# Second attention of a gated cross-attention block: the last keys' products of two head groups issued together

## The chip, the cores and the metric

The kernel runs on one core of one Trainium2 chip. The metric is the device time of one execution in microseconds (us); lower is better. Three timed runs of the kernel before gave 1540.47, 1540.97 and 1542.29 us; their median, 1540.97 us, is the time that counts. A separate execution was recorded by the hardware profiler, and every row quoted here comes from it.

## The reference, cut to what matters

The model adds four blocks to `x` (4 batches, 512 tokens, width 512, all float32): an attention, a mixture of experts, a second attention and a second mixture of experts. The change lies in the second attention. It has 16 heads of 32 columns over 512 context rows; the first 496 are ordinary keys, and the last 16 (`DCA`) form an attention of their own, with a softmax of their own, whose result is added:

```python
kv_dca = (y_dca @ Wkv_dca + bkv_dca).reshape(b, DCA, 2, H, HD)
k_dca = _ln(kv_dca[:, :, 0], kn_dca_w, kn_dca_b)
v_dca = kv_dca[:, :, 1]
...
ctx = _attn(qT, k.transpose(0, 2, 1, 3), v.transpose(0, 2, 1, 3))
ctx_dca = _attn(qT, k_dca.transpose(0, 2, 1, 3), v_dca.transpose(0, 2, 1, 3))
ctx = ctx + DCA_WEIGHT * ctx_dca
return ctx @ Wo + bo
```

## The kernel before, in words

The 16 heads are worked in four groups `g` of four heads, so a group fills 128 partitions. A slot is one batch `b`, one group `g` and one block `c` of 128 keys: 4 x 4 x 4 = 64 slots. TensorE does each slot in this order: `exponents` (`sc`, the scores of the slot, four products of 32 rows side by side; ScalarE makes `pt` from them), `weighted` (`o`, values times the `pt` of the slot before), some steps of other jobs, `maxima` of five slots ahead (`m`, scores again, from which VectorE takes the negated row maxima `nm`, two reductions, L1554), and more steps of other jobs. `sc` and `m` share one tag of PSUM tiles (two tiles of two banks each), so the first half of `sc` waits for the first `nm` reduction of the `m` before it, and its second half for the second. `acc` on GpSimd (L1595, L1598) sums the `pt` of a group over its four blocks.

The other jobs are Python generators. The table `WHEN` says at which half slots each is advanced; an even number is the place before `maxima`, an odd one the place behind it. At each place `go` advances every job twice, first the vector parts, then the products. All four engines issue in the order written (`manual_schedule`), so an instruction that waits holds everything behind it on its engine. The jobs share three single PSUM banks through `bank(name)` (`open_psum("psum1", 3)`): a fourth tile waits until the readers of one of the three have finished. Jobs that matter here: `queries` (`q`, `qT`, `d`), `keys`, `values`, `normed` (its transposes `xlnT`), `shared` (the shared expert's `gu` and `po`), `output` (`y`) and `normalized`.

`normalized(b, g)` finishes a group in seven places, 8, 9, 10, 11, 12, 15 and 16 half slots after the group's first slot: the sums `s` of the exponents, a copy, two reciprocals, the multiplication on GpSimd (L1636), then at place 15 (behind `maxima`) the product `dv` (L1641) and at place 16, in the next slot, VectorE's `scalar_tensor_tensor` (L1649), which adds `dv` and a bias to `q_t[:, g, :]`. `dv` is one float32 product with 64 contraction rows: the shares `pd_t` of the last keys are stored so that even groups lie on partitions 0 to 63 and odd groups on 64 to 127. `output` multiplies all four groups of `q_t` by `Wo` after the batch's last group.

Of the kernel before, what the change touches and what calls it, by code (L numbers as in the profile page):

```python
# [14 lines left out]
ALU = mybir.AluOpType  # L15
# [3 lines left out]
P = 128  # L19
# [60 lines left out]
C_BV = C_RMS + NC  # L80
# [6 lines left out]
def kernel(  # L87
# [32 lines left out]
    nc = tc.nc  # L120
# [14 lines left out]
    def bank(name):  # L135
        return phase[0].tile([P, 512], FP, tag="bank", bufs=phase[1], name=name)
# [18 lines left out]
    cols_sb = const.tile([P, N_COLS], FP, tag="cols", name="cols_sb")  # L155
# [375 lines left out]
    with tc.tile_pool(name="att0", bufs=2, reuse_waits="tile") as wk:  # L531
# [228 lines left out]
        b = B - 1  # L760
# [124 lines left out]
    vd_bd = wp1.tile([P, B, D], FP, tag="vd_bd", name="vd_bd")  # L885
# [337 lines left out]
    with tc.tile_pool(name="att1", bufs=1, reuse_waits="tile") as wk:  # L1223
# [18 lines left out]
        def nothing():  # L1242

            yield
            yield
# [372 lines left out]
        def normalized(b, g):  # L1618
            it = batches[b]
            q = it.q_t[:, g, :]  # L1620
            yield
            ps = bank(f"s_{b}_{g}")
            for j in range(4):
                nc.tensor.matmul(
                    ps[j * HD : (j + 1) * HD, :], lhsT=ones, rhs=it.acc[g][:, j, :], start=True, stop=True
                )
            yield
            rs = wk.tile([P, S], FP, tag="rs", name=f"rs_{b}_{g}")
            nc.scalar.copy(rs, ps)
            yield from nothing()  # L1630
            nc.vector.reciprocal(rs[:, : S // 2], rs[:, : S // 2])
            yield from nothing()
            nc.vector.reciprocal(rs[:, S // 2 :], rs[:, S // 2 :])
            yield from nothing()

            nc.gpsimd.tensor_tensor(q, q, rs, ALU.mult)  # L1636
            yield from nothing()
            rows_of = slice(g % 2 * 64, g % 2 * 64 + 64)
            yield
            pv = bank(f"dv_{b}_{g}")  # L1640
            nc.tensor.matmul(  # L1641
                pv,
                lhsT=vd_bd[rows_of, b, g * P : (g + 1) * P],
                rhs=it.pd_t[rows_of, g // 2, :],
                start=True,
                stop=True,
            )
            yield
            nc.vector.scalar_tensor_tensor(  # L1649
                q, pv, cols_sb[:, C_BV + g : C_BV + g + 1], q, ALU.add, ALU.add  # L1650
            )
            yield from nothing()

        def output(b, t):
# [76 lines left out]
        with tc.manual_schedule(engines={E.PE, E.DVE, E.Activation, E.Pool}):  # L1731
# [15 lines left out]
            for k, b in itertools.product(WHEN, range(B)):  # L1747
                first = per * b
                f = first - per
                if k == "normalized":  # L1750
                    for g in range(NC):
                        plan(first + g * TB, WHEN[k], normalized(b, g))
# [20 lines left out]
                elif k == "shifted":  # L1773
                    for g in range(NC):
                        f = first + g * TB
# [55 lines left out]
    with tc.tile_pool(name="exp1", bufs=1, side="right", reuse_waits="tile") as wk:  # L1831
# [60 lines left out]
        with tc.tile_pool(name="route1", bufs=1, reuse_waits="tile") as rp:  # L1892
# [50 lines left out]
            for h in range(8):  # L1943
                k, i0 = h // 4, h % 4 * n
# [4 lines left out]
                for i in range(n):  # L1949
                    nc.tensor.matmul(  # L1950
                        pi,
                        lhsT=hot_r[:, i, :],
                        rhs=hot_c[:, i].rearrange("p z s -> p (z s)"),
                        start=(h == 0 and i == 0),
                        stop=(h == 7 and i == n - 1),
# [145 lines left out]
```

## Time and profile before

| | |
|---|---|
| median of 3 runs | 1540.97 us (1540.47 to 1542.29) |
| profiled execution, its own time | 1549.78 us |
| its span, first to last instruction | 1548.0 us |
| TensorE busy | 1467.6 us (95%), granted clock 0.961 on average |
| VectorE, ScalarE, GpSimd busy | 647.3, 460.4, 577.7 us |
| the 16 `dv` products, busy | 18.0 us, first at 769.0 us, last at 1234.6 us |

The profiled execution is 8.81 us longer than the median of the runs. The page gives busy time by engine, the chain of work that ended last and the costliest groups; the trace answers with instructions in order of time (start, duration, engine, line, operation, tiles; in brackets the idle time before it and what ended it), with waits, and with busy time and granted TensorE clock for stretches of time. A float32 product shows as two matrix-multiply records. Records of matrix multiplies overlap a little at their ends, so the time that one takes in the queue is read from its start to the start of the next.

### The profile page before, as it was taken

What the parts mean: (1) busy time and instruction counts of PE and PEld (TensorE: products, weight loads), DVE (VectorE), ACT (ScalarE), POOL (GpSimd) and SP (SyncE); (2) the same over time, 40 slices, a digit from 0 to 9 for tenths busy, and PEclk for the clock granted to TensorE, in tenths of its full rate; (3) what the DMA queues carried; (4) which work ended last, traced back from release to release, by engine and by line L of the source; (5) the groups of instructions that cost most, each with busy time, mean ns of one, the idle gap of its engine ahead of it and who ended that gap; (6) DMA issues with size and microseconds to landing.
All of it is one profiled execution on the core that took longest, in us unless ns stands there. A gap on an engine that the chain in (4) does not pass through costs nothing.

```text
span 1548.0 us, 15460 instructions
## 1 busy us (share of the span) xinstructions
PE 1467.6 (95%) x5728; PEld 713.2 (46%) x5728; DVE 647.3 (42%) x1244; ACT 460.4 (30%) x722; POOL 577.7 (37%) x488
## 2 busy tenths in 40 slices
PE   7999899999999999798989999999999998899996
PEld 2454366665665666353233333333334354444443
DVE  3764422323312210255575566566654337222221
ACT  2553211111211111144454444543625211122221
POOL 0000121222232221136558576575665510344442
PEclk7999999999999999899999999998899998999998
DMA  9313424452443422410000000000000128444543
GB/s 329 106 75 132 137 44 115 109 133 62 106 136 69 116 63 34 117 69 15 0 1 1 0 1 14 27 2 1 28 28 21 61 108 328 102 87 93 94 88 46
DMA packets 60084, 119.89 MB, mean 77 GB/s; under 512 B 10401, under 2 KB 12961, under 8 KB 58977
## 3 DMA queue, kind: packets, MB, share of 16 engines
q0 software_dynamic: 17024, 40.17, 14.0%
q1 hardware_dynamic: 35872, 64.86, 12.1%
q10 hardware_dynamic: 7104, 13.78, 2.4%
q8 instruction: 49, 0.80, 0.2%
q14 instruction: 35, 0.28, 0.1%
HBM read 80.90 MB, written 37.89 MB: 77 GB/s over the span
## 4 chain that ended last, share of the span: by engine, by line
PE 80%; POOL 6%; DVE 4%; DMA 4%; issue 2%; ACT 2%; SPq 0%; POOLq 0%; ACTq 0%; DVEq 0%
PE gu_s L1117 18%; PE y_s L1134 8%; PE gu_s L408 8%; PE sc L1532 5%; PE m L1532 4%; PE y_s L432 4%; PE y L1268 3%; PE xm L651 3%; PE q L1268 3%; PE o L1608 3%; PE gu L1268 2%; POOL acc L1598 2%; ACT pt L1590 1%; PE v L1268 1%; PE k L1268 1%
## 5 line engine op out<-in xcount | busy, mean ns | idle before, releaser
L1554 DVE TENSOR_REDUCE nm<-m 128x2 f32<-128x992 f32 x128 | 146.3, 1185 | 142.4 <-PE m L1532 142.3
L1590 ACT ACTIVATE pt<-sc 128x1024 f32<-128x1024 f32 (+1 forms) x128 | 124.8, 1021 | 180.9 <-PE sc L1532 162.9
L1143 POOL DMA_INDIRECT sum<-y_s,idx x40 | 63.3, 1582 | 287.7 <-ACT y_s L1142 272.0
L1598 POOL TENSOR_TENSOR acc<-acc,pt 128x2048 f32<-128x2048 f32 (+1 forms) x32 | 144.4, 4511 | 60.7 <-ACT pt L1590 60.7
L1117 PE MATMUL gu_s<-h_t_s,wg 128*128 128x384 f32 (+1 forms) x512 | 150.8, 438 | 1.3 <-DVE h_t_s L1107 0.8
L1117 PE MATMUL gu_s<-h_t_s,wu 128*128 128x384 f32 (+1 forms) x512 | 148.3, 433 | 0.0
L1134 PE MATMUL y_s<-wd,mid_t_s 128*128 128x512 f32 x320 | 143.6, 592 | 0.0
L1128 DVE TENSOR_TENSOR mid_t_s<-act_s,gu_s 128x256 f32<-128x256 f32 (+1 forms) x64 | 31.2, 488 | 257.4 <-ACT act_s L1127 257.4
L408 PE MATMUL gu_s<-wgu,h_t_s 128*128 x288 | 132.1, 602 | 0.0
L1093 POOL DMA_INDIRECT got_s<-table,idx x40 | 40.0, 1001 | 230.6 <-PE lora_d L495 174.9
L1117 PEld LDWEIGHTS gu_s<-h_t_s,wu 128*128 128x128 f32 x512 | 97.7, 191 | 40.4
L1117 PEld LDWEIGHTS gu_s<-h_t_s,wg 128*128 128x128 f32 x512 | 94.9, 193 | 37.4 <-DVE h_t_s L1107 1.2
L1532 PE MATMUL sc<-xT,k_t 32*128 32x512 f32 (+1 forms) x512 | 100.2, 671 | 10.1 <-DVE nm L1554 7.7
L1595 POOL TENSOR_TENSOR acc<-pt,pt 128x2048 f32<-128x2048 f32 x16 | 72.2, 4512 | 94.8 <-ACT pt L1590 94.8
L1127 ACT ACTIVATE act_s<-gu_s 128x256 f32<-128x256 f32 (+1 forms) x64 | 27.9, 437 | 264.9 <-PE gu_s L1117 264.9
L437 POOL DMA_INDIRECT out<-y_s,idx x36 | 57.0, 1584 | 122.1 <-ACT mid_t_s L426 114.5
L1134 PEld LDWEIGHTS y_s<-wd,mid_t_s 128*128 128x128 f32 x320 | 60.9, 190 | 63.8 <-issue 57.6
L1532 PE MATMUL m<-k_t,xT 32*128 32x496 f32 x512 | 88.7, 674 | 1.7 <-ACT pt L1590 1.7
L408 PEld LDWEIGHTS gu_s<-wgu,h_t_s 128*128 128x128 f32 x288 | 52.9, 194 | 53.3 <-issue 53.3
L1608 PE MATMUL o<-pt,v 128*32 128x512 f32 (+1 forms) x512 | 73.4, 647 | 0.0
L432 PE MATMUL y_s<-wd,mid_t_s 128*128 x144 | 67.8, 593 | 0.8 <-ACT mid_t_s L426 0.8
L1142 ACT ACTIVATE y_s<-y_s,w_s 128x512 f32<-128x512 f32 x40 | 27.5, 687 | 121.6 <-PE y_s L1134 118.8
(370 smaller groups left out, 2099.3 us busy)
## 6 DMA issues: line engine op xcount, KB each, us to landing
wg<-in_wg SPq DMA_DIRECT2D x8, 1024.0 KB, 6.2
wu<-in_wu SPq DMA_DIRECT2D x8, 1024.0 KB, 7.0
wd<-in_wd SPq DMA_DIRECT2D x8, 1024.0 KB, 5.4
table<-xln SPq DMA_DIRECT2D x32, 256.0 KB, 2.0
wgu<-in_wgu ACTq DMA_DIRECT2D x2, 4096.0 KB, 15.4
ctx<-in_ctx_t SPq DMA_DIRECT2D x8, 512.0 KB, 6.8
x_sb<-in_x SPq DMA_DIRECT2D x4, 1024.0 KB, 13.9
sum<-x_sb SPq DMA_DIRECT2D x16, 256.0 KB, 2.0
```

The lines of the kernel that those rows point to most:

```text
L408: nc.tensor.matmul(gu[:, k * n : (k + 1) * n], lhsT=t.h_t[:, c, :], rhs=t.gate_up(c)[k], start=(c == 0), stop=(c == NC - 1),)
L432: nc.tensor.matmul(py, lhsT=t.mid_t[:, f, :], rhs=t.down(f), start=(f == 0), stop=(f == nf - 1))
L1117: nc.tensor.matmul(gu[:, k, :n], lhsT=w[:, c, f * P : (f + 1) * P], rhs=g.h_t[:, c, :n], start=(c == 0), stop=(c == NC - 1),)
L1134: nc.tensor.matmul(py, lhsT=g.mid_t[:, f, a * P : (a + 1) * P], rhs=wd[:, f, :], start=(f == 0), stop=(f == F0 // P - 1),)
L1143: nc.gpsimd.indirect_dma_start(out=sum0[:, :], out_offset=bass.IndirectOffsetOnAxis(ap=slots_of(g, a), axis=0), in_=y, in_offset=None, com ...
L1268: nc.tensor.matmul(pp, lhsT=lhs(c), rhs=w[:, c, :], start=(c == 0), stop=(c == n - 1))
L1532: nc.tensor.matmul(halves[j // 2][:n, j % 2, :width], lhsT=lhs(rs), rhs=rhs(rs), start=True, stop=True,)
L1554: nc.vector.tensor_reduce(it.nm[g][:, t, 2 * k : 2 * k + 2], m[:, :, :S2], AX.X, ALU.max, negate=True)
L1590: nc.scalar.activation(it.pt[:n, 2 * k : 2 * k + 2, :], sc[:n], AF.Exp)
L1595: nc.gpsimd.tensor_tensor(acc, it.pt0, it.pt, ALU.add)
L1598: nc.gpsimd.tensor_tensor(acc[:n], acc[:n], it.pt[:n], ALU.add)
L1608: nc.tensor.matmul(it.po[j * HD : (j + 1) * HD, :], lhsT=it.v[:n, c, h * HD : (h + 1) * HD], rhs=pt[:n, j, :], start=(c == 0), stop=(c == ...
```

## The change

Groups are finished in pairs. For an even `g` the generator keeps its places but issues neither product nor addition. For an odd `g` it issues at place 15 the products of `g - 1` and `g` one behind the other, each into its own bank, on rows 0 to 63 and 64 to 127 of the array, and at place 16 the two additions. The number of instructions stays as it was; only the order on TensorE and VectorE and the lifetime of the banks differ.

```diff
-            rows_of = slice(g % 2 * 64, g % 2 * 64 + 64)
-            yield
-            pv = bank(f"dv_{b}_{g}")
-            nc.tensor.matmul(
-                pv,
-                lhsT=vd_bd[rows_of, b, g * P : (g + 1) * P],
-                rhs=it.pd_t[rows_of, g // 2, :],
-                start=True,
-                stop=True,
-            )
-            yield
-            nc.vector.scalar_tensor_tensor(
-                q, pv, cols_sb[:, C_BV + g : C_BV + g + 1], q, ALU.add, ALU.add
-            )
+            yield
+            both = []
+            for k in (g - 1, g) if g % 2 else ():
+                rows_of = slice(k % 2 * 64, k % 2 * 64 + 64)
+                pv = bank(f"dv_{b}_{k}")
+                nc.tensor.matmul(
+                    pv,
+                    lhsT=vd_bd[rows_of, b, k * P : (k + 1) * P],
+                    rhs=it.pd_t[rows_of, k // 2, :],
+                    start=True,
+                    stop=True,
+                )
+                both.append((k, pv))
+            yield
+            for k, pv in both:
+                q = it.q_t[:, k, :]
+                nc.vector.scalar_tensor_tensor(
+                    q, pv, cols_sb[:, C_BV + k : C_BV + k + 1], q, ALU.add, ALU.add
+                )
             yield from nothing()
```

## The prediction, made before the changed kernel was run

> **What bounds the kernel now.** I read the page's busy times and chain first, then the waits of TensorE in the stretch of the second attention (755 to 1240 us), then the rows of `dv`, then all 16 places of `dv` in order of time.
>
> ```profile
> PE 1467.6 (95%) x5728; PEld 713.2 (46%) x5728; DVE 647.3 (42%) x1244; ACT 460.4 (30%) x722; POOL 577.7 (37%) x488
> PE 80%; POOL 6%; DVE 4%; DMA 4%; issue 2%; ACT 2%; SPq 0%; POOLq 0%; ACTq 0%; DVEq 0%
> PE sc L1532 <- DVE nm L1554: 7.7, 8, 3.8
> L1641 PE MATMUL dv<-pd_t,vd_bd x32: 589/641/694, 769.0 to 1235.2; 64*128 64x512 f32 x32
> L1649 DVE SCALAR_TENSOR_TENSOR xT<-dv,cols_sb,xT x16: 721/743/751, 771.3 to 1237.4; 128x512 f32<-128x512 f32 x16
> ```
>
> TensorE carries the span, which makes a product saved look like time saved. But its longest wait here is `sc` for `nm`, and `dv` stands just between `m` and `sc`, so each place must be read alone.
>
> **What the pair saves on TensorE.** One `dv` holds the queue 1.05 us (1186.27 to 1187.32 below). Two products side by side are shown by half an `sc`: at 770.36 two row groups of 32 run together, and the other half starts at 771.45, 1.09 us later. So a pair costs what one costs, and the eight even `dv` are freed: 8 x 1.05 = 8.4 us, if nothing else holds what follows. The second addition (0.74 us) moves to the odd places; VectorE idles 1.3 us before the next `nm` at 807.03, 934.39 and 1063.32, so it costs nothing there; without that idle time it would cost 0.74 at each.
>
> **The eight even places: where the 8.4 us go.** First group of batch 0:
>
> ```profile
> 767.17 1.90 PE L1532 MATMUL m<-k_t,xT 32*128 32x496 f32 x8
> 769.00 1.12 PE L1641 MATMUL dv<-pd_t,vd_bd 64*128 64x512 f32 x2
> 770.36 2.22 PE L1532 MATMUL sc<-xT,k_t 32*128 32x512 f32 x8 [0.24 <-DVE nm L1554]
> 769.12 2.29 DVE L1554 TENSOR_REDUCE nm<-m 128x2 f32<-128x992 f32 x2 [1.14 <-PE m L1532]
> ```
>
> `nm` ends at 770.31 and 771.41; the halves of `sc` start right after. Taking `dv` out opens a hole and moves nothing: 0. The same at 893.17 (`sc` at 894.53, `nm` until 894.47 and 895.57). At 826.71 and 1084.32 the first half of `sc` comes 0.3 us sooner, but the second still waits for `nm` until 828.55 and 1086.16: 0. Third batch:
>
> ```profile
> 1022.10 1.98 PE L1268 MATMUL y<-wo_sb,xT 128*128 128x512 f32 x4
> 1024.01 1.12 PE L1641 MATMUL dv<-pd_t,vd_bd 64*128 64x512 f32 x2
> 1025.07 1.14 PE L1532 MATMUL sc<-xT,k_t 32*128 32x512 f32 x8
> 1022.20 2.29 DVE L1554 TENSOR_REDUCE nm<-m 128x2 f32<-128x992 f32 x2 [2.07 <-PE m L1532]
> ```
>
> Here a `y` also stands between, and `nm` ends at 1023.39 and 1024.49. The second half could start at 1024.54 instead of 1025.07: 0.5 saved. At 1150.79 the same numbers (`nm` until 1151.27, `sc` at 1151.85): 0.5. At 957.28 also 0.5, but TensorE then waits at 963.40 for `xln` from GpSimd, which has run since 954.71: 0. At 1222.44 no `m` is left, but the `s` at 1227.45 waits for `acc` (GpSimd, 1222.88 to 1227.41): 0. Sum of the even places: -1.0 us of 8.4.
>
> **The odd places: banks.** A pair takes two of the three banks. Going through all tiles in the written order, five pairs find their banks free: in the traces their predecessors' readers end at least 0.2 us before (799.20 against 799.97, 927.05 against 927.33, for instance). Three don't.
>
> Batch 3, group 1 (1186.27). `shared` holds two banks here: `gu` of the next batch, read two slots later, and a `gu` whose second half is multiplied behind the pair. So the second `dv` can only take the first one's bank, after its addition.
>
> ```profile
> 1186.27 1.12 PE L1641 MATMUL dv<-pd_t,vd_bd 64*128 64x512 f32 x2
> 1187.32 1.14 PE L1532 MATMUL sc<-xT,k_t 32*128 32x512 f32 x8
> 1187.50 0.75 DVE L1649 SCALAR_TENSOR_TENSOR xT<-dv,cols_sb,xT 128x512 f32<-128x512 f32 x1 [5.58 <-POOL acc L1598]
> ```
>
> The addition ends at 1188.25; the second `dv` starts at 1188.30 and ends its turn at 1189.35; `sc` would have started at 1187.32. Queued behind it on TensorE are `sc`, `o`, `gu`, and everything after: +2.0.
>
> Batch 2, group 3 (1113.71): two transposed tiles `xlnT` follow the pair, the fourth tile for three banks. Its four transposes wait for the addition:
>
> ```profile
> 1114.76 1.09 PE L922 MATMUL xlnT<-ident,xln 128*128 128x128 f32 x8
> 1115.79 1.14 PE L1532 MATMUL sc<-xT,k_t 32*128 32x512 f32 x8
> 1115.20 0.72 DVE L1649 SCALAR_TENSOR_TENSOR xT<-dv,cols_sb,xT 128x512 f32<-128x512 f32 x1
> ```
>
> The addition ends at 1115.93, behind the two `nm`; four transposes take 0.5; `sc` starts at 1116.5 instead of 1115.79: +0.7.
>
> Batch 3, group 3 (1234.63): the three banks hold `po` tiles. The pair takes those read by 1231.99 and 1234.29; `y` now needs the third, read by the addition at 1235.86, in place of one that was free.
>
> ```profile
> 1235.68 14.00 PE L1268 MATMUL y<-wo_sb,xT 128*128 128x512 f32 x32
> 1235.86 0.65 DVE L1719 SCALAR_TENSOR_TENSOR x_sb<-po,tg,x_sb 128x512 f32<-128x512 f32 x1
> ```
>
> That ends at 1236.51, so `y` starts at 1236.55: +0.8. All three lie on stretches where the chain runs over TensorE, so the waits are passed on. Banks: +3.5. Their floor is 0 (a reader that comes sooner); the ceiling is twice as much, should the scheduler's choice among banks be worse. [...]
>
> **The clock.** The holes are new, and a hole can slow the clock:
>
> ```profile
> 1064.57 3.11 PE L1532 MATMUL sc<-xT,k_t 32*128 32x512 f32 x8 [0.99 <-DVE nm L1554]
> 1062.36:1065.77 3.41, 2.42 (x14) 0.82 (x12) 2.45 (x3) 1.64 (x5) 0.00 (x0) 1.00 0.00 0
> 1065.77:1072.60 6.83, 6.83 (x22) 1.70 (x23) 3.62 (x6) 2.05 (x2) 3.72 (x1) 0.50 0.00 0
> ```
>
> The third value from the end (1.00, 0.50) is the granted clock. A hole of 0.99 us between `m` and an `sc` that came by halves was followed by 6.83 us at half clock: `sc` 3.11 instead of 2.22, `o` 1.94 instead of 1.07, `m` 2.04 instead of 1.11, `y` 2.54 instead of 1.99, together 3.2 us, or 1.6 for each 3.41 us. The change widens just such holes: to 1.29 us at 769.07 and 1.28 at 893.25, to 0.7 at 1084.39 (and one at 826.8, which lies under GpSimd's work). Holes of 0.98 at 1226.47 and 1.41 at 961.99, with full-width work around them, were not followed by a slow clock; 0.24 at 770 and 894 neither. So between none and three stretches of 6.83 us: 0 to +9.6. I take an even chance for each of the three and the shorter length, 1.5 x 1.6 = +2.4, since the 1062 hole is nearest in kind but not certain to repeat.
>
> [...]
>
> **Sum.** -1.0 + 3.5 + 2.4 = +4.9 us on the profiled execution's 1549.78. That execution is 8.81 us above the median; carried over, 1540.97 + 4.9 = 1545.9 us. About 0.2%, 3.1 us, is what a measurement of this kernel can tell from no change.
>
> **The rivals.**
> - *Banks without the clock.* The holes don't slow the clock: -1.0 + 3.5 = +2.5, 1543.5 us, inside 0.2%. For it: most short holes in this trace went unpunished. Chance 0.28.
> - *The pair doesn't run side by side* (the change doesn't do what it says). Two 64-row products then hold the queue 2.1 us. At 799.97, 861.57, 927.33, 990.49 and 1056.26 `nm` is over before `sc`, so each costs 1.05; the three bank places hide most of it (+0.5 together): 4.9 + 5.8 = +10.7 at worst with the clock, +8.3 without; 1549 to 1551.7 us. Against it: the halves of `sc`. Chance 0.10.
> - *Faster: the even places pass their time on.* Place: the queue between `m` and `sc`. If `nm` weren't late there, each freed `dv` would be worth its 1.05 us: -8.4 + 3.5 = -4.9, 1536.1 us. It decides where the second `nm` ends before TensorE is through with the work left between; that holds at 957, 1024 and 1150 only by half. For it: TensorE's 80% of the chain. Chance 0.10.
> - *My case*, holes, banks and one or two slow stretches: 0.52; its own range 1544 to 1549.
>
> **How the numbers follow.** The likeliest case gives 1545.9. The range 1540.0 to 1551.5 takes in the case without the clock, the bank floor, and most of the serial pair; it leaves out the faster case and the upper edge of the serial one, about 0.17. Faster by over 0.2%: 0.09, nearly all of that rival. Within: 0.33, the case without the clock and the low edge of mine. Slower: 0.58.
>
> **What would show it.** Right: pairs of `dv` starting within 0.1 us of each other at seven places and 2.0 us apart at batch 3, group 1; `sc` waiting about 1.2 us for `nm` in the first slots of batches 0 and 1 (waits of `sc` for `nm` above 7.7 us); the transposes split by a wait in batch 2, group 3; `y` held for `po`; half-clock stretches near 772, 895 or 1086 us. Wrong: `dv` pairs 1.05 us apart everywhere (serial), or `m`, `nm` and `sc` of batches 0 and 1 closing up so that the slots there get shorter by a microsecond each (faster).

## The result, and the profile after

The changed kernel is slower: 1548.95 us (median of 19 runs) beside 1542.29 us for the kernel before in the same rounds (19 runs), a ratio of 1.0034, 95% interval 1.0022 to 1.0046. That is +5.2 us (+3.4 to +7.1); the two medians lie 6.7 us apart, since the runs of each kernel spread over some 10 us, and the text goes by the ratio. The forecast was +4.9 us. Its profiled execution took 1553.01 us with a span of 1551.3 us, near the upper end of its runs. All times of the experiments below stand beside runs of the kernel before on the same chip in the same rounds.

The page of the changed kernel, busy times and chain of waits:

```profile
PE 1466.8 (95%) x5728; PEld 712.8 (46%) x5728; DVE 651.2 (42%) x1244; ACT 460.7 (30%) x722; POOL 578.2 (37%) x488
PE 81%; POOL 5%; DVE 5%; DMA 3%; issue 2%; ACT 2%; SPq 0%; POOLq 0%; ACTq 0%; DVEq 0%
```

Little is to be seen here: the same instructions, busy for nearly the same time. The change shows in TensorE's waits in the stretch of the second attention (us in total, times, longest):

```profile
PE sc L1532 <- DVE nm L1554: 11.6, 11, 3.8
...
PE s L1624 <- POOL acc L1598: 2.0, 1, 2.0
...
PE xlnT L922 <- DVE xT L1656: 1.4, 1, 1.4
...
PE dv L1645 <- DVE xT L1656: 0.8, 1, 0.8
PE y L1268 <- DVE x_sb L1726: 0.8, 1, 0.8
```

The first line grew from 7.7 us in 8 times: where an even `dv` is gone, `sc` stands and waits for `nm`. The second is the hole before `s` in batch 3, which was 0.98 us. The last three are new, and each is a bank that isn't free. They are the three places that the prediction named. In the order of time, batch 2 group 3, then batch 3 group 1, then `y`:

```profile
1111.39 1.13 PE L1645 MATMUL dv<-pd_t,vd_bd 64*128 64x512 f32 x4
1111.50 2.29 DVE L1554 TENSOR_REDUCE nm<-m 128x2 f32<-128x992 f32 x2 [0.35 <-PE m L1532]
1112.45 0.66 PE L922 MATMUL xlnT<-ident,xln 128*128 128x128 f32 x4
1113.79 1.38 DVE L1656 SCALAR_TENSOR_TENSOR xT<-dv,cols_sb,xT 128x512 f32<-128x512 f32 x2
1114.57 0.66 PE L922 MATMUL xlnT<-ident,xln 128*128 128x128 f32 x4 [1.45 <-DVE xT L1656]
1115.15 1.14 PE L1532 MATMUL sc<-xT,k_t 32*128 32x512 f32 x8
...
1185.09 1.12 PE L1645 MATMUL dv<-pd_t,vd_bd 64*128 64x512 f32 x2
1186.25 0.75 DVE L1656 SCALAR_TENSOR_TENSOR xT<-dv,cols_sb,xT 128x512 f32<-128x512 f32 x1 [5.51 <-PE dv L1645]
1187.06 1.12 PE L1645 MATMUL dv<-pd_t,vd_bd 64*128 64x512 f32 x2 [0.85 <-DVE xT L1656]
1188.11 2.09 PE L1532 MATMUL sc<-xT,k_t 32*128 32x512 f32 x8
...
1238.94 2.41 PE L1268 MATMUL y<-wo_sb,xT 128*128 128x512 f32 x5 [0.81 <-DVE x_sb L1726]
```

`dv ... x4` in 1.13 us is a pair side by side (four records, two products). It stands so at seven of the eight odd places; at 1185.09 and 1187.06 the two products are 1.97 us apart. The same rows of before have `sc` 2.08 us behind `dv` in batch 2 group 3 (1113.71 to 1115.79), here 3.76; and 1.05 in batch 3 group 1, here 3.02.

### The profile page after: what moved, and what is told of

Its sections match the earlier page's. It is cut to its first block, busy times and chain, and to the rows that moved or that the text cites. A ratio compares the mean times of both kernels' runs of the same rounds, so it can differ in the third digit from the quotient of the medians.

```text
span 1551.3 us, 15443 instructions
## 1 busy us (share of the span) xinstructions
PE 1466.8 (95%) x5728; PEld 712.8 (46%) x5728; DVE 651.2 (42%) x1244; ACT 460.7 (30%) x722; POOL 578.2 (37%) x488
## 4 chain that ended last, share of the span: by engine, by line
PE 81%; POOL 5%; DVE 5%; DMA 3%; issue 2%; ACT 2%; SPq 0%; POOLq 0%; ACTq 0%; DVEq 0%
PE gu_s L1117 18%; PE y_s L1134 8%; PE gu_s L408 8%; PE sc L1532 5%; PE y_s L432 4%; PE m L1532 4%; PE xm L651 4%; PE y L1268 3%; PE q L1268 3%; PE o L1608 3%; PE gu L1268 2%; PE v L1268 2%; POOL acc L1595 2%; POOL acc L1598 1%; ACT pt L1590 1%
## 5 line engine op out<-in xcount | busy, mean ns | idle before, releaser
L408 PE MATMUL gu_s<-wgu,h_t_s 128*128 x288 | 131.9, 601 | 0.0
L1532 PE MATMUL m<-k_t,xT 32*128 32x496 f32 x512 | 84.6, 653 | 1.5 <-ACT pt L1590 1.5
L408 PEld LDWEIGHTS gu_s<-wgu,h_t_s 128*128 128x128 f32 x288 | 52.8, 193 | 53.3 <-issue 53.3
```

The costliest lines, as they stand in the source:

```text
L408: nc.tensor.matmul(gu[:, k * n : (k + 1) * n], lhsT=t.h_t[:, c, :], rhs=t.gate_up(c)[k], start=(c == 0), stop=(c == NC - 1),)
L1532: nc.tensor.matmul(halves[j // 2][:n, j % 2, :width], lhsT=lhs(rs), rhs=rhs(rs), start=True, stop=True,)
```

## The experiments

The theory: an even `dv` is hidden behind `nm`, so freeing it gives next to nothing; the pairs wait for banks at three places; and half-clock stretches behind the new holes cost the rest. Rivals: the loss is all banks and no clock; the loss is all clock; TensorE's amount of work sets the time after all.

In the traces I follow the start of every `exponents` step against the same step in the profile of before. Before the second attention the executions already lie up to 10 us apart, so only changes of this shift within the attention are read. Half-clock stretches that move from one execution to the next put 1.6 us or more on such a shift (the one of 3.41 us at 771.69 us in the changed kernel, which before lacks, put 1.6 on it), so small terms are read at their own place.

**Five pairs, three pairs.** The pairs are kept only at the five places where no bank is missed, or only at the other three; the remaining groups are finished singly, as before.

```diff
-            for k in (g - 1, g) if g % 2 else ():
+            paired = (b, g // 2) in ((0, 0), (0, 1), (1, 0), (1, 1), (2, 0))
+            for k in ((g - 1, g) if g % 2 else ()) if paired else (g,):
```

In the second kernel the list is `((2, 1), (3, 0), (3, 1))`.

> Pairs at the five places where three banks suffice, single products as before at batch 2 groups 2 and 3 and all of batch 3. My account (banks and holes): the three bank waits (3.5 us) go, so 4 us below the changed kernel and within 0.1% of the kernel before: -0.5 for the even place at 1024 us, and up to +1.6 from slow clock after the holes at 769 and 893 us. Rival, holes alone: the bank waits are not passed on, and it stays some 0.25% slower than before. No wait of dv, xlnT or y for a bank in the trace.

> The complement: pairs at batch 2 groups 2 and 3 and in batch 3 alone, the places with the bank waits. My account: +3.5 us of bank waits, -0.5 for the even place at 1150 us, and 0 to 3 us of slow clock after the holes at 1084 us and in front of the last sums: 1541 + 4 us, most of the change's loss. Rival, holes alone: only the hole at 1084 is left, +1 us or less.

Five pairs: 1543.32 us, ratio 0.9994 (0.9972 to 1.0016), no wait for a bank in the trace, and the 0.5 us at 1024 us is gained (shift -0.54). Three pairs: 1550.27 us, ratio 1.0045 (1.0029 to 1.0062), about +6.9 us. The loss goes with the three places where a bank is missed; a pair as such costs nothing that these runs can tell from 0 (0.9972 to 1.0016).

**Holes filled.** A spare product with 64 rows that nobody reads stands at each even place, where the single `dv` stood. The pairs stay.

```diff
+            if g % 2 == 0:
+                nc.tensor.matmul(
+                    bank(f"spare_{b}_{g}"),
+                    lhsT=vd_bd[0:64, b, g * P : (g + 1) * P],
+                    rhs=it.pd_t[0:64, g // 2, :],
...
```

> The changed kernel with a product of the same shape, never read, at each even place, so that the holes are filled as before. Banks and holes: the bank waits stay, +3.5 us on the kernel before; the 1.0 us saved at even places is given back, the slow stretches near 772 and 829 us vanish: 1.5 us below the changed kernel or level with it, although TensorE does 8 products more. Rival, banks alone (holes cost nothing): 1.0 us above the changed kernel, +6 on the kernel before.

1550.39 us, ratio 1.0031 (1.0012 to 1.0050): level with the changed kernel. The bank waits are all there. So the holes carry little of the loss, or as much as the even places give back; the time alone doesn't separate the two.

**Even products left out.** The even groups' product and addition are left out altogether, so the output lacks the last keys' share of these groups; odd groups are single.

```diff
-            for k in (g - 1, g) if g % 2 else ():
+            for k in (g,) if g % 2 else ():
```

> The products and additions of the even groups are left out altogether (their share of the last keys is missing from the output), the odd ones stand single as before: the best that any pairing at the odd places could give. My account: -1.0 us, and up to +2.4 from slow clock after the holes: between 1540 and 1543 us where the kernel before has 1541, although eight products and eight additions are gone. Rival, TensorE-bound: 8 x 1.05 = -8.4 us, 0.55% faster.

1542.46 us, ratio 0.9996 (0.9978 to 1.0014). Eight products fewer (8.4 us of TensorE's queue) and eight additions fewer are worth about 0 (-3.4 to +2.2 us). The rival on TensorE's amount of work wanted -8.4 us and falls.

**All products left out** (the last keys' share is missing for every group).

> All 16 products and their additions are left out (the output lacks the last keys' part): what the whole step holds up. My account from the rows of before: the even places give 1.0 us; of the odd ones, those ahead of more TensorE work (800, 862, 927, 990, 1056 us) 0.5 each, where sc then meets the end of the second nm, 1186 us the full 1.05, 1114 us 0.5, 1235 us none, as y waits for the last multiplication on GpSimd: about -5 us, 0.3% faster, less 1.6 us of slow clock in front of the last sums. Rival, TensorE-bound: 16 x 1.05 = -16.8 us, 1.1% faster.

1571.84 us, ratio 1.0188 (1.0166 to 1.0210), which says nothing on TensorE: the output feeds the routing of the second mixture of experts, and a block that runs only when the tokens need more tiles than usual ran at the end. The timeline there shows its start:

```profile
1535.76 1.94 PE L390 MATMUL gotT_s<-ident,got_s 128*128 128x128 f32 x8 [10.47 <-DMA got_s<-table,idx]
```

With it come 24 more records of the gate and up products (312 instead of 288 on L408). Within the attention the 16 missing products bring about -4 us, read from the shift, not -16.8; that much stays readable, the whole time does not.

**One left out, one filled.** The hole before `s` in batch 3 by itself. These two kernels and the two behind them ran once each, for the profile (1543.47, 1541.20, 1543.79 and 1543.89 us); one time says nothing about a few microseconds here, so only the traces are used. In the first kernel all groups are single and only batch 3 group 2 is left out (its share of the last keys is missing); the second is the changed kernel with a spare product at that one place.

```diff
-            for k in (g - 1, g) if g % 2 else ():
+            for k in (g,) if (b, g) != (3, 2) else ():
```

```diff
+            if (b, g) == (3, 2):
+                nc.tensor.matmul(
+                    bank(f"spare_{b}_{g}"),
...
```

> All products single as before, and the one of batch 3, group 2 left out with its addition (its share is missing from the output). If the hole ahead of the last sums slows the clock: s waits 2.0 us instead of 1.0 for acc, a stretch of 3.41 us at half clock begins within 8 us behind it, and from the last exponents to the first y the trace takes 1.6 us longer than before's 24.7. Rival, holes cost nothing: no such stretch, the same 24.7 us.

> The changed kernel with one product of the same shape, never read, at the place of batch 3, group 2. If the hole slows the clock: no half-clock stretch ahead of the last sums, and 0.9 us more than before from the last exponents to the first y (the bank wait of y alone), where the changed kernel took 2.5 more. Rival: 2.5 more as in the changed kernel, or above.

Filled, the stretch from the last `exponents` step (1217.5 us in the changed kernel) to the first `y` is 0.9 us longer than before, the bank of `y` alone. In the changed kernel it is 2.5 us longer. The other 1.6 us follow the hole. The changed kernel ahead of its half-clock stretch and in it (window in us; busy time of PE, PEld, DVE, ACT, POOL with counts; granted clock; DMA share; GB/s):

```profile
1225.66:1229.07 3.41, 1.38 (x10) 0.16 (x8) 0.75 (x1) 0.00 (x0) 2.49 (x1) 1.00 0.21 77
1229.07:1232.49 3.42, 3.42 (x14) 2.44 (x11) 1.38 (x2) 0.59 (x1) 0.00 (x0) 0.50 0.00 0
```

TensorE idles 2.03 us of the first 3.41 us, all of the hole, and the 3.42 us behind them have half the clock. But "one left out", which has the same hole of 2.04 us, missed what I expected: no slow stretch, and no 1.6 us. Around its hole and behind it:

```profile
1215.74:1219.16 3.42, 2.99 (x13) 0.83 (x12) 1.07 (x2) 0.59 (x1) 3.42 (x2) 1.00 0.21 78
1219.16:1222.57 3.41, 1.80 (x15) 0.96 (x16) 0.47 (x2) 0.59 (x1) 1.56 (x1) 1.00 0.21 77
1222.57:1225.98 3.41, 3.41 (x11) 1.66 (x10) 2.54 (x4) 0.00 (x0) 0.00 (x0) 1.00 0.00 0
```

The granted clock stays at 1.00 throughout. The other traces with this hole part in the same way. "Three pairs" and "even products left out" (2.03 us each) are slowed behind it: the eight records of `xlnT` that come next take 1.97 us, as in the changed kernel. In "all left out" and "one left out" (2.04 us each) they take 1.09, as before. From the last `exponents` step to the first `y` it is 20.55 us in "even products left out", 18.93 in "one left out" and 18.93 before. Three times slow and two not: the same hole was followed by a loss of 1.6 us or by none, and what decides it these runs don't show.

Idle time alone doesn't tell the two apart. In the changed kernel half clock also follows 3.42 us with 0.72 us idle (826.30 to 829.72) and 3.41 us with none (1119.85 to 1123.26).

**One pair in batch 2 group 3, one pair in batch 3 group 1.** The two larger bank terms, each by itself; the list `paired` holds only `(2, 1)` or only `(3, 0)`.

> Only groups 2 and 3 of batch 2 are a pair, all others as before. Bank theory, resized by the traces: the four transposes xlnT behind the pair wait for the addition, and the queue from the odd dv to the next sc takes 3.4 to 3.8 us instead of 2.07: +1.3 to +1.7 us on the exponents that follow, where the prediction had +0.7; the even place of batch 2, group 2 gives back 0.5 only if the scores there start sooner, which they don't without the product left out at group 0 (0). Rival, the banks hardly matter and the loss is the clock's: +0.3 or less from dv to sc at this place. Read from the profile alone.

> Only groups 0 and 1 of batch 3 are a pair, all others as before. Bank theory: the two dv stand 2.0 us apart and sc starts 2.0 us later than one place behind a single dv, +1.9 us on the exponents of the next slot; the even place of group 0 gives -0.5 before that. No wait of xlnT or y. Rival, the banks hardly matter: the two dv within 0.1 us of each other and no shift. Read from the profile alone.

Batch 2 group 3, first where it is the pair, then, as the control, where the same place is single:

```profile
1104.25 1.13 PE L1646 MATMUL dv<-pd_t,vd_bd 64*128 64x512 f32 x4
...
1107.43 0.66 PE L922 MATMUL xlnT<-ident,xln 128*128 128x128 f32 x4 [1.46 <-DVE xT L1657]
...
1108.02 1.14 PE L1532 MATMUL sc<-xT,k_t 32*128 32x512 f32 x8
1109.09 1.06 PE L1608 MATMUL o<-pt,v 112*32 112x512 f32 x8
```

```profile
1104.77 1.12 PE L1646 MATMUL dv<-pd_t,vd_bd 64*128 64x512 f32 x2
...
1106.85 1.50 PE L1532 MATMUL sc<-xT,k_t 32*128 32x512 f32 x8
...
1108.28 1.06 PE L1608 MATMUL o<-pt,v 112*32 112x512 f32 x8
```

From `dv` to `sc` it is 3.77 us instead of 2.08 (+1.7); to `o`, since the single one's `sc` waits for `nm` with its second half, 4.84 instead of 3.51 (+1.3). So the term is 1.3 to 1.7 us, as the resized theory had it, and not 0.7.

What is left of it two slots later is another matter. A half-clock stretch follows this place in every trace (at 1123.80 us before, at 1123.26 in the changed kernel), and its length differs. From the exponents ahead of the place to those two slots on, three traces with the pair here ("one pair", "three pairs", "holes filled") take 24.8 us, and the stretch lasts 6.83 us; the other two, the changed kernel and "one filled", take 21.9, and it lasts 3.41. With a single `dv` at this place the six traces of the experiments take 21.8 to 22.2 us. So behind this place the wait cost 3 us in three traces and nothing in two, one of them the changed kernel's.

In batch 3 group 1 the second kernel has its two `dv` 1.97 us apart, and the shift goes from -9.15 to -7.19 at the next slot: +1.96, as expected. A half-clock stretch of 6.83 us follows 10 us later, which put another 1.5 us on it. Whether the wait brings that stretch on stays open: in the changed kernel, with the same wait, one of 3.41 us begins at 1188.12 us, 1.06 us behind the start of the second `dv`, and before, without the wait, one of 3.41 us at 1198.89; one of 6.83 us stands in "holes filled" with the wait, but also in "all left out" without it.

**The pair in the hole.** The traces point to a version that could gain. The places worth having are not those of groups 0 and 2, where `sc` waits for `nm` anyway, but that of group 1, where the prediction's second rival noted that `nm` is over before `sc`. So groups 0 and 3 stay single, and group 1 waits for group 2, at whose place there is room.

```diff
-            for k in (g - 1, g) if g % 2 else ():
+            for k in ((0,), (), (1, 2), (3,))[g]:
```

> The pair the other way round: group 0 and group 3 single as before, groups 1 and 2 together at the place of group 2. The products that go are those of group 1; the pair stands where nm, GpSimd or a bank's reader is late anyway, and two banks are free there by the written order. My account: -0.5 each at 800, 927 and 1056 us, -1.05 at 1186 us, no bank wait, and the product at 1222 us stays: -2.6 us, ratio 0.998 to 0.999. Rival, any pair perturbs the order and costs: above 1.001.

> The same kernel as the pair in the hole (groups 0 and 3 single, groups 1 and 2 together at the place of group 2), run again: ratio 0.9957 to 0.9995 as before, about 0.998 (-3 us). If the gain was scatter of the rounds, the interval takes in 1 with its middle within 0.001 of it.

First time 1538.68 us beside 1542.97, ratio 0.9976 (0.9957 to 0.9995); again 1538.06 beside 1541.61, ratio 0.9972 (0.9956 to 0.9988): about -4 us, faster than both kernels. The freed place in batch 3 group 1, where `sc` follows `gu` at once:

```profile
1169.98 5.32 PE L1268 MATMUL gu<-xT,shared_gu 128*128 128x512 f32 x12
...
1175.23 1.14 PE L1532 MATMUL sc<-xT,k_t 32*128 32x512 f32 x8
```

Of the shifts, this place gives -1.05 us; those of batches 0, 1 and 2 give about -0.6, -0.54 and -0.5 (a microsecond at once, of which half comes back in the next slots). Together -2.7. `sc` waits for `nm` no longer than before (7.8 and 7.4 us), and no bank is missed. Both its traces also lack two half-clock stretches that others have (3.41 us each, at 1045.29 and 1198.89 us before and at 1044.76 and 1188.12 in the changed kernel; about 1.6 us of time each), so part of the gain may be the clock's; why they are missing stays open.

## Why the prediction was right

**The even places** came out as worked out. At 769 us a hole opens and nothing moves (predicted hole 1.29 us):

```profile
768.35 2.29 DVE L1554 TENSOR_REDUCE nm<-m 128x2 f32<-128x992 f32 x2 [1.27 <-PE m L1532]
769.59 2.22 PE L1532 MATMUL sc<-xT,k_t 32*128 32x512 f32 x8 [1.28 <-DVE nm L1554]
```

At 1024 and 1150 us the shift falls by 0.53 and 0.54 us (predicted 0.5 each), also in "even products left out". At the other five places that I put at 0 before batch 3's last, the shift is the same behind them as ahead, but for the half-clock stretch at 772 us, of which below. At 957 us, for one, the next exponents come 1.05 us sooner and all of it is given back one slot later, as GpSimd's cover would have it.

**The eighth even place, 1222 us,** was the step that failed. I put it at 0, because `s` waits for `acc`. It does, but in the changed kernel the longer hole was followed by 3.42 us at half clock, which cost 1.6 us. In "one left out" the same hole cost nothing, so 0 was one of two outcomes.

**The pair side by side:** right, 1.13 us for four records.

**The banks:** all three places, and no fourth. Of the sizes, +2.0 (batch 3 group 1) measured 1.97, and +0.8 (`y`) measured 0.8 to 0.9. The term of +0.7 (batch 2 group 3) was undersized by 0.6 to 1.0 us. I read the addition's end from the profile of before, where `nm` began 0.8 us ahead of `dv` (1112.92 against 1113.71). In that execution `m` had come in two parts; in the changed kernel `m` came whole, `nm` began at 1111.50, behind `dv` at 1111.39, and the first addition, which stands behind `nm`, came that much later. In all 11 other traces that have a `dv` here `nm` begins 0.1 us behind it as well. The row that I chose was the exception among the ways in which this place runs, and I took it for the only one.

**The clock:** +2.4 at 769, 893 and 1084 us was wrong in its places. Nothing followed at 893 and 1084. The slow stretch at 1065.77 us that I went by shows in no other trace; in the changed kernel the same hole, 1.00 us ahead of `sc` at 1064.45, was not followed by one. At 827 us, in the hole that I had put under GpSimd's work, a half-clock stretch of 3.41 us did follow, from 829.72 us: so in all five traces without that product, in none of the eight with it. It cost nothing, as the shift is 0.24 ahead and 0.22 behind. At 772 us a half-clock stretch came too, and put 1.6 us on what follows; but it came in every other trace too, at the same work, among them "holes filled", "the pair in the hole" and "one left out", where a product stands in that hole. Only the profile of before lacks the stretch. So these runs don't put it down to the hole. What the holes cost in this trace was 1.6 us at a place that I hadn't counted.

By place, the terms measured are -1.07 (even places) + 1.97 + 1.5 + 0.85 (banks; the middle one is between 1.3 and 1.7) + 1.6 (clock) = +4.9 us. So the total of the forecast was right partly by luck: the banks were 0.8 too small and the clock 0.8 too large, and 1.6 for the clock is what the one profiled execution of this kernel showed; how many of the 19 runs paid it isn't known. With -0.53 for the place at 1150 us, which alone is free in "three pairs", the same sum gives +5.4 there (measured +4.5 to +9.6), without clock and even places +4.3 in "holes filled" (+1.9 to +7.7), and 0.5 in "even products left out" (-3.4 to +2.2).

This sum adds the waits, each at its own place. Over the whole stretch from the first exponents to the first `y` behind the last the traces take 526.1 us (before), 530.5 (changed), 526.7 ("one left out"), 528.4 ("one filled"), 533.6 ("three pairs") and 534.1 ("holes filled"): half-clock stretches that come, go or change their length, as behind batch 2 group 3, move them by up to 3 us about the sums. That 4.9 forecast, 4.9 by place and 5.2 measured lie so close is therefore luck as well. What the runs show is that the loss goes with the three bank places, and what each of the three waits is.

**The rivals.** "Banks without the clock", +2.5, was smaller than the interval's lower end, +3.4. With the banks as measured it would be +3.3, so the times alone don't exclude it; against it stand the slow records of `xlnT` behind the hole in three of the traces. "Not side by side" falls with the rows of `dv`. "Faster" falls with "even products left out": `nm` was late at the even places, all but the two halves named.

## What to carry to other kernels

A product saved is worth its time only where the next instruction on its engine would be ready; read that at each place, and move work out of places where the next instruction waits for nobody into those where it does. Two products that share the array save queue time (1.06 us for the pair here, 1.05 for one) but hold two banks at once; with few banks, three here, walk through the tiles in issue order and see whose reader must now end sooner. Where one profiled execution prices a wait, look whether the instructions ahead of it could come in another order, and take both prices.

## What the hardware showed that was not expected

- A hole of 2.03 us in TensorE's work was followed by 3.42 us at a granted clock of 0.50 in the changed kernel, and by equally slow records in two more traces (`xlnT` 1.97 us); holes of 2.04 us at the same place in two others were not (1.09 us). So for the same instructions the hole came to 1.6 us or nothing, and idle time didn't tell which: half clock also followed 3.41 us without any (1119.85 to 1123.26).
- Two float32 products of 64 rows and 512 columns in different row halves of the array held the queue as long as one does: `dv` to the next product 1.06 us for the pair (1111.39 to 1112.45), 1.05 for one (1113.71 to 1114.76 before).
- Leaving out part of an attention changed the routing of the mixture of experts behind it, and with it the time, by +29 us (1571.84 beside 1542.97), although the attention itself was some 4 us shorter: an experiment that leaves work out ahead of data-dependent control flow must be read by stage.
